# Moving a second norm and part of an edge gather from a tail into the attention before it

## The chip, the cores and the metric

The kernel runs on one core of a Trainium2 chip. The metric is the time of one execution on the device, in microseconds (us). The kernel before was timed three times: 15623.67, 15634.05 and 15639.06 us, median 15634.05. A separate execution was recorded by the hardware profiler; it took 15643.13 us, and its trace spans 15641.4 us.

The engines are named as the profile names them: PE multiplies matrices, DVE is the vector engine, ACT the engine for activation functions, POOL the general-purpose engine (it issues the indirect gathers here), SP the engine that issues the other transfers. Each works through its own queue in program order.

## The reference

The input is four entries of 32 x 96 tokens with 256 features, 3072 tokens per entry and 12288 in all.

- Layer 0 is a group norm, then two Mamba scans (over the 96 positions, then over the 32 variables), and a residual.
- Layer 1 normalizes each token and runs an additive attention within each entry: `e[i,j] = Wa . tanh(q_i + k_j + bh)` with 32 hidden units, a softmax over j, and the sum of the normalized tokens. The result is added to the tokens.
- Then each token is normalized a second time, and a graph part follows: `h = x W_gat` gives 4 heads x 4 experts per token. For each of 1048576 edges (and a loop at each token) a score is formed:

```
e = leaky_relu(a_src[src] + a_dst[dst])
alpha = softmax of e over the edges that share dst
agg[dst] = sum of alpha * h[src]
```

  The edge indices of the reference run over 65536 nodes, and there are only 12288 tokens here. Destinations beyond the tokens are dropped and sources beyond them are clamped to the last token. So few edges need a gather; the rest is counted.
- `agg` is normalized, averaged over heads, the best two of four experts get softmax weights, and each token's output is the weighted sum of expert networks `gelu(x W1 + b1) W2 + b2` (256 to 512 to 256), added to the tokens.

## The kernel before

`whole` (L1701) writes one program in an order fixed by hand for PE, ACT, DVE and POOL (`manual_schedule`); Python generators are advanced in turn, and what each emits lands in the engines' queues in that order.

**The attention.** `Attention.units` (L771) walks 3072 slots, 768 for each entry. In a slot, one `th` (L790, ACT) computes tanh for four queries against all 3072 keys, and PE multiplies an earlier slot's `th` by the weight into scores (L766). Eight slots make a unit of 32 queries, and four units a tile of 128 queries: an entry has 24 tiles of 32 slots. `tile_tail` (L867) ends a tile in six steps, one per slot: `factors`, `factors2`, `factors3` (ACT, `f`, L903), `spread` (POOL, four `sf`, L907), `together` (PE, `po`, L912, needs `sf`) and `outputs` (DVE, and the store of the tile's rows to `x2`). So a tile's end depends on POOL, and PE, in order, meets `po` right behind the scores of a slot.

**The second norm.** `after(b)` (L927) reads an entry's `x2` back in 12 pairs of tiles. It takes inverse roots of all variances with one square root on ACT (L675), and for each pair it normalizes (L680), transposes on PE (L694), stores `xn2T`, multiplies by `W_gat` (L948), forms both score vectors on DVE (L952 to L958) and stores them to the tables `tab_s` (source scores and features, 20 numbers a token) and `tab_a` (destination scores, 4 numbers). For entries 0 to 2 this runs beside the next entry's attention, one step in a slot that has no other use of the one shared PSUM bank (`beside`). For entry 3 it runs after the last attention.

**Beside the attention of the last entries.** `Edges.sort` (L1027) compacts the edge lists on DVE; it ends with the copy of `cnt` (L1162), and then the expert weights are loaded. The list has four parts, one for each entry of the destination, with 108 columns of 128 edges each: `si` and `di` hold the rows of the tables to gather. From the last entry on, `Experts.early` (L1435) computes expert units whose gates are not yet known and keeps the products in DRAM (`kept`). A unit is one expert on one block of 512 tokens. While `after(3)` runs behind the last attention, each of its steps is followed by four steps of early units (L1809).

**The tail.** `tail` (L1518) does the remaining expert units, three steps a unit, with the graph part planned by step number (`at`). `Graph.tables` (L1202) loads both tables, takes the maximum source score over all partitions (`topa`, L1216, POOL) and computes the shift of each destination, `leaky(a_dst + max)`; the score and the shift go to a third table, `tab_d`, 8 numbers a token, which is stored to DRAM. `Graph.gather` (L1245) fetches 12 columns with 24 indirect transfers issued by POOL (L1253), alternately `gs` from `tab_s` and `gd` from `tab_d`, one per column. There are 36 such groups, in the order of entries 3, 2, 0, 1; group m is emitted at step 12 + 4m. Ten steps later `scores` (L1260) forms the weights, `spread` (L1270) builds one-hot matrices (`ol`, `oh`) and products (`rh`, L1284), and `place` (L1289) sums them with PE (`pa`, L1294) into one bank for the entry. After nine groups `finish` (L1299) makes the gates of an entry. Four `gs` and four `gd` buffers exist, so a gather waits for the scores four groups back. A block whose gates are late has its products kept and added afterwards (L1503, `y<-all`).

Of the kernel before, what the change touches and what calls it, by code (L numbers as in the profile page):

```python
# [26 lines left out]
P = 128  # L27
# [17 lines left out]
KQ = TOK // NQT  # L45
LAG = 2
# [15 lines left out]
G0, PART = 4, 8  # L62
# [560 lines left out]
class Attention:  # L623
# [303 lines left out]
    def after(self, b):  # L927

        nc, mv = self.nc, self.state[b]["mv2"]
        N = NT // CT  # L930
        x2 = self.x2[b * TOK:(b + 1) * TOK, :]
        x = self.tiles_of(x2, 0)
        rs = self.inverse_roots(mv)
        yield
        for j in range(N):
# [27 lines left out]
            nc.sync.dma_start(self.tab_a[:, n0:n0 + CT, :], db)  # L963
# [3 lines left out]
class Edges:  # L967
# [6 lines left out]
    def __init__(self, ctx, tc, a):  # L974
# [8 lines left out]
        self.nc.sync.dma_start(self.lanes, a["lanes"])  # L983

# [51 lines left out]
    def sort(self):  # L1036
# [4 lines left out]
        with ExitStack() as ctx:  # L1041
# [124 lines left out]
class Graph:  # L1166
# [4 lines left out]
    def __init__(self, ctx, tc, a, ed, tab_s, tab_a, tab_d, gates):  # L1171
        self.nc, self.ed = tc.nc, ed
        self.tab_s, self.tab_a, self.tab_d, self.gates = tab_s, tab_a, tab_d, gates
# [28 lines left out]
    def tables(self):  # L1202
# [3 lines left out]
        adst = new("adst", [P, NH, 2 * HEADS])  # L1206
        nc.sync.dma_start(hall, self.tab_s)
        nc.sync.dma_start(adst[:, :, 0:HEADS], self.tab_a)
# [5 lines left out]
        top, topa = new("top", [P, HEADS]), new("topa", [P, HEADS])  # L1214
        nc.vector.tensor_reduce(top, hall[:, :, 0:HEADS].rearrange("p n h -> p h n"), AX.X, ALU.max)
# [5 lines left out]
        nc.sync.dma_start(self.tab_d, adst)  # L1221
# [23 lines left out]
    def gather(self, j):  # L1245
        nc, ed = self.nc, self.ed
        gs = self.wk.tile([P, GP, ROW], F32, tag="gs", name="gs", bufs=4)
        gd = self.wk.tile([P, GP, 2 * HEADS], F32, tag="gd", name="gd", bufs=4)
        q, c0 = divmod(j * GP, CQ)
        rows = lambda t: t.rearrange("p n f -> (p n) f")  # L1250
        for u in range(GP):
            for to, table, idx in ((gs, self.tab_s, ed.si), (gd, self.tab_d, ed.di)):
                nc.gpsimd.indirect_dma_start(  # L1253
                    out=to[:, u, :], out_offset=None, in_=rows(table),
                    in_offset=bass.IndirectOffsetOnAxis(ap=idx[:, q, c0 + u:c0 + u + 1], axis=0))
        self.got[j] = gs, gd

    def scores(self, j):
        nc = self.nc
        gs, gd = self.got.pop(j)  # L1260
        e = self.wk.tile([P, GP, HEADS], F32, tag="e", name="e")
        v = self.wk.tile([P, GP, ROW], F32, tag="v", name="v")
        nc.vector.tensor_tensor(e, gs[:, :, 0:HEADS], gd[:, :, 0:HEADS], ALU.add)
        self.leaky(e)
        nc.vector.tensor_tensor(e, e, gd[:, :, HEADS:], ALU.subtract)
# [252 lines left out]
def tail(tc, a, ed, ex, w, tab_s, tab_a, tab_d, gates):  # L1518


    with ExitStack() as ctx:
        gr = Graph(ctx, tc, a, ed, tab_s, tab_a, tab_d, gates)
        ex.open(ctx, w)
        gr.tables()
# [28 lines left out]


# [53 lines left out]
def general_tail(tc, a, x2, xn2T, tab_s, tab_a, tab_d, gates, out, dram):  # L1608

    nc = tc.nc  # L1610
    with ExitStack() as ctx:
# [3 lines left out]
        gr = Graph(gctx, tc, a, none, tab_s, tab_a, tab_d, gates)  # L1615
# [6 lines left out]
        gr.tables()  # L1622
        for _ in gr.own_edges():
            pass
# [77 lines left out]
def whole(tc, a, dram, out):  # L1702
# [10 lines left out]
    tab_a = dram.tile([P, NH, HEADS], F32, tag="tab_a", name="tab_a")  # L1713
    tab_d = dram.tile([P, NH, 2 * HEADS], F32, tag="tab_d", name="tab_d")
    with ExitStack() as ctx:
        actx, lctx, ectx = ExitStack(), ExitStack(), ExitStack()
        with tc.manual_schedule(engines={E.PE, E.Activation, E.DVE, E.Pool}):
# [9 lines left out]
            def steps():  # L1727
# [11 lines left out]
                lists, units = ed.sort(), None  # L1739

                us_v = us_t = 0.0
                while True:
                    us_v = min(us_v, 0.0) + EDGE_US
                    while lists and us_v > 0 and len(ed.todo) < 2:
                        us = next(lists, None)
                        if us is None:
                            lists = None
                            late["w"] = Experts.weights(
                                ectx.enter_context(tc.tile_pool(name="late2", bufs=1)), nc, a)
# [32 lines left out]
            tables = x2, xn2T, tab_s, tab_a, tab_d, late["gates"], out  # L1782
            tail(tc, a, late["ed"], late["ex"], late["w"], *tables[2:6])
# [81 lines left out]
```

## Time and profile before

| what | value |
| --- | --- |
| median of three runs | 15634.05 us |
| the profiled execution's own time | 15643.13 us |
| span of its trace | 15641.4 us |
| PE, DVE, ACT, POOL busy over the span | 75%, 71%, 77%, 58% |
| `cnt` copied, the sort's end | 13617.6 us |
| last score matmul of the attention (L766) | ends near 13991 us |
| first gather of the tail | 14227.4 us |
| last gather of the tail | 15481.3 us |
| last matmul | ends near 15613.9 us |

All times count from the start of the span. The span falls into four stretches that matter here: the work up to the sort's end, the last tiles of the attention (13617 to 14004), the stretch in which only the second norm of entry 3 and early units run (14004 to 14225), and the tail (14225 to the end). A busy share over the whole span mixes them, so each is read alone.

### The profile page before, as it was taken

Reading aid. Unit: us, or ns where it says so; the run is one execution under the profiler, and the core shown is the slowest. Engines: PE = TensorE matmul, PEld = TensorE weight load, DVE = VectorE, ACT = ScalarE, POOL = GpSimd, SP = SyncE. Lnnn points to the kernel's source line nnn. Section 1 sums busy time; section 2 is a strip of 40 time slices with the busy share of each in tenths; the row PEclk is TensorE's granted clock in tenths of the full one; section 3 lists DMA queues with packets and bytes.
Section 4 is the critical chain, followed back from the end, with each engine's and each line's share of the span. In section 5 each row is a group of like instructions: output and inputs, shape, how many; then the busy total and the mean of one; then the engine's idle time right before and its main releaser. Section 6 shows DMA issues by size and latency. Waiting matters only on the chain.

```text
span 15641.4 us, 222408 instructions
## 1 busy us (share of the span) xinstructions
PE 11808.2 (75%) x85872; PEld 5087.3 (33%) x85872; DVE 11045.8 (71%) x15303; ACT 12053.9 (77%) x9331; POOL 9052.0 (58%) x6586
## 2 busy tenths in 40 slices
PE   5666665777777767777777777777778788889988
PEld 2222222222222232222223322222233344446545
DVE  7888888777777787777778876777677733323455
ACT  3443335999999979999998899999979899971211
POOL 4555557777777767777777675777500000004774
PEclk8888886888888888888888888888889999999999
DMA  5666665444445444444444443454310000013223
GB/s 188 203 202 203 199 198 160 149 145 151 148 146 150 154 151 145 145 148 147 148 149 150 151 147 115 143 152 151 121 47 28 17 8 8 21 36 82 43 62 101
DMA packets 1168144, 1959.71 MB, mean 125 GB/s; under 512 B 408545, under 2 KB 612961, under 8 KB 1164897
## 3 DMA queue, kind: packets, MB, share of 16 engines
q1 hardware_dynamic: 1139424, 1939.16, 39.8%
q0 software_dynamic: 27648, 6.25, 0.8%
q8 instruction: 675, 11.06, 0.3%
q14 instruction: 397, 3.24, 0.1%
HBM read 1841.73 MB, written 103.28 MB: 124 GB/s over the span
## 4 chain that ended last, share of the span: by engine, by line
ACT 37%; PE 20%; DVE 17%; POOL 12%; issue 10%; DMA 4%; SPq 0%; DVEq 0%; POOLq 0%; ACTq 0%
ACT th L790 27%; PE pe L766 9%; DVE h L388 6%; ACT dA L371 6%; POOL h L395 4%; POOL gs L1253 3%; POOL gd L1253 3%; PE pv L857 2%; DVE dB L379 2%; ACT pr L841 2%; DMA bB<-bc 2%; PE ptw L848 1%; PE po L1432 1%; POOL ub L305 1%; PE ph L1424 1%
## 5 line engine op out<-in xcount | busy, mean ns | idle before, releaser
L790 ACT ACTIVATE th<-krep,qsel 128x3072 f32<-128x3072 f32 x3072 | 8666.3, 2848 | 327.1 <-PE pe L766 309.7
L766 PE MATMUL pe<-th,wa_blk 128*32 128x384 f32 x49152 | 5118.1, 547 | 1893.1 <-ACT pr L841 1536.3
L395 POOL TENSOR_TENSOR h<-h,bC 128x768 f32<-128x768 f32 x2048 | 3785.0, 1848 | 2561.5 <-DVE h L388 2310.8
L388 DVE TENSOR_TENSOR_SCAN h<-dA,dB 128x384 f32<-128x384 f32 x4096 | 3683.3, 940 | 787.4 <-ACT dA L371 601.8
L766 PEld LDWEIGHTS pe<-th,wa_blk 128*32 128x32 f32 x49152 | 1472.2, 118 | 4581.0 <-issue 1989.1
L379 DVE TENSOR_TENSOR dB<-bB,dtu 128x768 f32<-128x768 f32 x2048 | 1946.2, 950 | 131.7 <-DMA bB<-bc 87.5
L371 ACT ACTIVATE dA<-dt,t_A 128x380 f32<-128x380 f32 x2048 | 1122.1, 570 | 879.6 <-DVE h L388 873.9
L907 POOL TENSOR_SCALAR sf<-sel,f 128x32 f32<-128x32 f32 x384 | 152.5, 421 | 2639.2 <-ACT f L903 2522.0
L371 ACT ACTIVATE dA<-dt,d_A 128x372 f32<-128x372 f32 x2048 | 1097.8, 562 | 557.3 <-DVE h L388 551.8
L414 PE MATMUL py<-h,ident 128*128 128x384 f32 x2176 | 1000.6, 592 | 680.0 <-POOL h L395 678.7
L402 POOL TENSOR_TENSOR h<-h 128x768 f32<-128x768 f32 x752 | 1422.9, 1892 | 46.6
L850 DVE COPY pT<-ptw 128x512 f32<-128x512 f32 (+1 forms) x768 | 425.7, 554 | 1149.6 <-PE ptw L848 1148.4
L857 PE MATMUL pv<-xn,pT 128*32 128x257 f32 x18432 | 1090.6, 384 | 84.3 <-DVE pT L850 83.5
L414 PEld LDWEIGHTS py<-h,ident 128*128 128x128 f32 x2176 | 438.1, 219 | 1243.8 <-POOL h L395 1016.1
L403 POOL TENSOR_TENSOR h<-h 128x384 f32<-128x384 f32 x752 | 803.0, 1068 | 59.0
L404 POOL TENSOR_TENSOR y<-y,h 128x384 f32<-128x384 f32 x752 | 773.7, 1029 | 59.0
L857 PEld LDWEIGHTS pv<-xn,pT 128*32 128x32 f32 x18432 | 584.4, 111 | 638.3 <-DVE pT L850 169.5
L1500 ACT ACTIVATE h<-ph,b 128x512 f32<-128x512 f32 x248 | 165.2, 686 | 702.8 <-PE ph L1424 702.4
L1253 POOL DMA_INDIRECT gs<-tab_s,si x432 | 501.6, 1161 | 131.7 <-issue 127.1
L1253 POOL DMA_INDIRECT gd<-tab_d,di x432 | 487.3, 1128 | 134.7 <-issue 130.1
L309 DVE SCALAR_TENSOR_TENSOR ua<-ub,ua 128x384 f32<-128x384 f32 x256 | 429.2, 1677 | 190.5 <-POOL ub L305 186.3
L1432 PE MATMUL po<-w,h 128*128 128x256 f32 x1984 | 471.9, 393 | 54.7 <-DVE o L1493 38.4
(280 smaller groups left out, 14868.4 us busy)
## 6 DMA issues: line engine op xcount, KB each, us to landing
bB<-bc SPq DMA_DIRECT2D x2048, 384.0 KB
bC<-bc SPq DMA_DIRECT2D x2048, 384.0 KB
x<-x SPq DMA_DIRECT2D x144, 256.0 KB
kept<-ko SPq DMA_DIRECT2D x68, 512.0 KB
all<-kept SPq DMA_DIRECT2D x17, 2048.0 KB
xt<-xn2T SPq DMA_DIRECT2D x59, 512.0 KB
x<-x SPq DMA_DIRECT2D x192, 128.0 KB
xs<-in_xT SPq DMA_DIRECT2D x16, 768.0 KB
```

The lines of the kernel that those rows point to most:

```text
L371: nc.scalar.activation(inner(dA[:, :T]), inner(blk["dt"][:, e, :]), AF.Exp, scale=blk["w"]["A"][:, e, i + s:i + s + 1])
L379: nc.vector.tensor_tensor(dB, blk["bB"].pop(j), z["dtu"].unsqueeze(1).to_broadcast([P, SB, T]), ALU.mult)
L388: nc.vector.tensor_tensor_scan(h[:, s, :], z.pop(("dA", e, i + s))[:, :T], z["dB"][:, s, :], 0.0, ALU.mult, ALU.add)
L395: nc.gpsimd.tensor_tensor(h, h, blk["bC"].pop(j), ALU.mult)
L402: nc.gpsimd.tensor_tensor(h0, h0, h1, ALU.add)
L403: nc.gpsimd.tensor_tensor(h0[:, 0, :], h0[:, 0, :], h0[:, 1, :], ALU.add)
L404: nc.gpsimd.tensor_tensor(y[e], y[e], h0[:, 0, :], ALU.add)
L414: nc.tensor.matmul(z["py"], self.ident, h[:, s, :], start=(i == 0), stop=(i == DS - 1))
L766: nc.tensor.matmul(pe[q * QU:(q + 1) * QU, j, :KQ // 2], self.wa[:, k, :], th[:, c0:c0 + KQ // 2], start=(k == 0), stop=(k == NK - 1))
L790: nc.scalar.activation(th, s["krep"], AF.Tanh, bias=s["qsel"][:, col:col + 1])
L857: nc.tensor.matmul(pv[q * QU:(q + 1) * QU, :C + 1], pT[:, i, q * QU:(q + 1) * QU], s["xn"][:, q * NK + i, :], start=(i == 0), stop=(i == N ...
L1253: nc.gpsimd.indirect_dma_start(out=to[:, u, :], out_offset=None, in_=rows(table), in_offset=bass.IndirectOffsetOnAxis(ap=idx[:, q, c0 + u: ...
```

## The change

1. **The last entry's second norm in four parts.** `after` takes a range of tiles. For entry 3 it is appended three times beside its own attention, for tiles 0 to 7, 8 to 15 and 16 to 21, twelve slots after the last slot of the part (slots 268, 524 and 716 of 768). Only tiles 22 and 23, one pair, are left for behind the attention. Each part takes its own square roots.
2. **Destination scores in a table per entry, without the shift.** `tab_a` becomes four DRAM tables, `tab_d` is not used in the normal case, and `di` becomes a row within an entry's table (four small DVE instructions more in the sort). The shift is formed after the gather, from the gathered score and `topa`, with two DVE instructions more for each group of 12 columns.
3. **Gathered beside the last attention.** `gd` becomes one tile for all 432 columns. When the sort has ended, each slot of the attention emits three gathers of entries 0, 1 and 2, until 324 are done. The 108 of entry 3 stay in the tail, beside their `gs`. So the tail issues 540 gathers in place of 864.
4. **Tail order.** Group 0 is gathered ahead of `tables`, group m at step 4m (m from 1), with scores at step 10 + 4m. `tables` is called after the plan has been laid out.

In the built programs the number of expert units done up to the last score matmul is the same: 20 complete, and the hidden half of the 21st. Behind it the kernel before does 13 hidden halves and 14 output halves more as early units and 62 units in the tail; the changed one does 3 and 4 more, and 72 in the tail. The blocks with kept products go from 17 to 14.

```diff
+AFTER = (0, 8), (8, 16), (16, 22), (22, 24)
-G0, PART = 4, 8
+G0, PART = 10, 8
-    def inverse_roots(self, mv):
+    def inverse_roots(self, mv, t0=0, t1=NT):
         rs = self.rows.tile([P, NT], F32, tag="lrs", name="lrs")
-        self.nc.scalar.activation(rs, mv[:, :, 1], AF.Sqrt, bias=self.eps)
-        self.nc.vector.reciprocal(rs, rs)
+        some = rs[:, t0:t1]
+        self.nc.scalar.activation(some, mv[:, t0:t1, 1], AF.Sqrt, bias=self.eps)
+        self.nc.vector.reciprocal(some, some)
...
-            if b and col == LAG + 10:
+            if b and col == LAG + 10 and b < B:
                 side.append(self.after(b - 1))
+            if b == B - 1:
+                side += [self.after(b, t0, t1) for t0, t1 in AFTER[:-1]
+                         if col == t1 * P // R_ATT + LAG + 10]
...
-        side.append(self.after(B - 1))
+        side.append(self.after(B - 1, *AFTER[-1]))
...
-            nc.sync.dma_start(self.tab_a[:, n0:n0 + CT, :], db)
+            nc.sync.dma_start(self.tab_a[b][:, j * CT:(j + 1) * CT, :], db)
...
+    def places(self, pool, tab_a):
+        self.gd = pool.tile([P, 4, CQ, HEADS], F32, tag="gd", name="gd")
+        self.tab_a, self.have = tab_a, set()
+
+    def gather(self, q, c):
+        if (q, c) not in self.have:
+            self.have.add((q, c))
+            self.nc.gpsimd.indirect_dma_start(
+                out=self.gd[:, q, c, :], out_offset=None,
+                in_=self.tab_a[q].rearrange("p n f -> (p n) f"),
+                in_offset=bass.IndirectOffsetOnAxis(ap=self.di[:, q, c:c + 1], axis=0))
...
+                if rows is self.di:
+                    v.tensor_scalar(lo, lo, float(NT) / NH, None, ALU.mult)
+                    for q in range(1, 4):
+                        part = hi[:, q * CQ:(q + 1) * CQ]
+                        v.tensor_scalar(part, part, float(-q * NT), 0.0, ALU.add, ALU.max)
...
-        nc.sync.dma_start(self.tab_d, adst)
...
         for u in range(GP):
-            for to, table, idx in ((gs, self.tab_s, ed.si), (gd, self.tab_d, ed.di)):
-                nc.gpsimd.indirect_dma_start(
-                    out=to[:, u, :], out_offset=None, in_=rows(table),
-                    in_offset=bass.IndirectOffsetOnAxis(ap=idx[:, q, c0 + u:c0 + u + 1], axis=0))
+            nc.gpsimd.indirect_dma_start(
+                out=gs[:, u, :], out_offset=None, in_=rows,
+                in_offset=bass.IndirectOffsetOnAxis(ap=ed.si[:, q, c0 + u:c0 + u + 1], axis=0))
+            ed.gather(q, c0 + u)
...
-        nc.vector.tensor_tensor(e, e, gd[:, :, HEADS:], ALU.subtract)
+        nc.vector.tensor_tensor(sh, gd, self.topa.unsqueeze(1).to_broadcast([P, GP, HEADS]), ALU.add)
+        self.leaky(sh)
+        nc.vector.tensor_tensor(e, e, sh, ALU.subtract)
...
-            t = 3 * G0 + PART * m // 2
-            at(t, lambda j=j: gr.gather(j))
-            t += 10
+            t = G0 + PART * m // 2
+            if m < 1:
+                gr.gather(j)
+            else:
+                at(max(0, t - 10), lambda j=j: gr.gather(j))
             at(t, lambda j=j: gr.scores(j))
...
+                            ed.places(pool, tab_a)
+                            columns = [(q, c) for q in range(B - 1) for c in range(CQ)]
...
                     while units and us_t > 0:
                         us_t -= next(units) or 0.0
+                    for _ in range(3 if columns else 0):
+                        ed.gather(*columns.pop(0))
                     yield
```

More of the change, by code (lines that the diff above doesn't have):

```diff
@@ L925, in tile_tail, with after @@
         return [factors, factors2, factors3, spread, together, outputs]
-    def after(self, b):
+    def after(self, b, t0=0, t1=NT):
         nc, mv = self.nc, self.state[b]["mv2"]
-        N = NT // CT
+        j0, N = t0 // CT, t1 // CT
         x2 = self.x2[b * TOK:(b + 1) * TOK, :]
-        x = self.tiles_of(x2, 0)
-        rs = self.inverse_roots(mv)
+        x = self.tiles_of(x2, j0)
+        rs = self.inverse_roots(mv, t0, t1)
         yield
-        for j in range(N):
+        for j in range(j0, N):
             rowsd = slice(b * TOK + j * CT * P, b * TOK + (j + 1) * CT * P)
@@ L1166, with __init__ @@
 class Graph:
-    def __init__(self, ctx, tc, a, ed, tab_s, tab_a, tab_d, gates):
+    def __init__(self, ctx, tc, a, ed, tab_s, tab_a, gates):
         self.nc, self.ed = tc.nc, ed
-        self.tab_s, self.tab_a, self.tab_d, self.gates = tab_s, tab_a, tab_d, gates
+        self.tab_s, self.tab_a, self.gates = tab_s, tab_a, gates
         pool = lambda name, bufs, **k: ctx.enter_context(tc.tile_pool(name=name, bufs=bufs, **k))
@@ L1205, in tables @@
         self.hall = hall = new("hall", [P, NH, ROW])
-        adst = new("adst", [P, NH, 2 * HEADS])
+        adst = self.adst = new("adst", [P, NH, 2 * HEADS])
         nc.sync.dma_start(hall, self.tab_s)
-        nc.sync.dma_start(adst[:, :, 0:HEADS], self.tab_a)
+        for q in range(4):
+            nc.sync.dma_start(adst[:, q * NT:(q + 1) * NT, 0:HEADS], self.tab_a[q])
         last = self.last = new("last", [P, ROW])
@@ L1214, in tables @@
         top, topa = new("top", [P, HEADS]), new("topa", [P, HEADS])
+        self.topa = topa
         nc.vector.tensor_reduce(top, hall[:, :, 0:HEADS].rearrange("p n h -> p h n"), AX.X, ALU.max)
@@ L1247, in gather @@
         gs = self.wk.tile([P, GP, ROW], F32, tag="gs", name="gs", bufs=4)
[L1248 removed]
         q, c0 = divmod(j * GP, CQ)
[L1250 removed]
+        rows = self.tab_s.rearrange("p n f -> (p n) f")
         for u in range(GP):
[L1252 to L1256 removed]
+            nc.gpsimd.indirect_dma_start(
+                out=gs[:, u, :], out_offset=None, in_=rows,
+                in_offset=bass.IndirectOffsetOnAxis(ap=ed.si[:, q, c0 + u:c0 + u + 1], axis=0))
+            ed.gather(q, c0 + u)
+        self.got[j] = gs
     def scores(self, j):
         nc = self.nc
[L1260 removed]
+        gs = self.got.pop(j)
+        q, c0 = divmod(j * GP, CQ)
+        gd = self.ed.gd[:, q, c0:c0 + GP, :]
         e = self.wk.tile([P, GP, HEADS], F32, tag="e", name="e")
+        sh = self.wk.tile([P, GP, HEADS], F32, tag="sh", name="sh")
         v = self.wk.tile([P, GP, ROW], F32, tag="v", name="v")
[L1263 removed]
+        nc.vector.tensor_tensor(e, gs[:, :, 0:HEADS], gd, ALU.add)
         self.leaky(e)
[L1265 removed]
+        nc.vector.tensor_tensor(sh, gd, self.topa.unsqueeze(1).to_broadcast([P, GP, HEADS]), ALU.add)
+        self.leaky(sh)
+        nc.vector.tensor_tensor(e, e, sh, ALU.subtract)
         self.weighted(e, v, gs[:, :, HEADS:], GP)
@@ L1515, in outputs_tile, with tail @@
         return self.io.tile([P, NQ, NEXP, C], F32, tag="all", name="all")
-def tail(tc, a, ed, ex, w, tab_s, tab_a, tab_d, gates):
+def tail(tc, a, ed, ex, w, tab_s, tab_a, gates):
     with ExitStack() as ctx:
-        gr = Graph(ctx, tc, a, ed, tab_s, tab_a, tab_d, gates)
+        gr = Graph(ctx, tc, a, ed, tab_s, tab_a, gates)
         ex.open(ctx, w)
-        gr.tables()
         PER = NBLK_X // B
@@ L1552, in tail @@
                 ready[q] = t + 5
+        gr.tables()
         first = {i: n for n, (i, e) in reversed(list(enumerate(units)))}
@@ L1605, in tail, with general_tail @@
                         ex.store(i, to[n - 1])
-def general_tail(tc, a, x2, xn2T, tab_s, tab_a, tab_d, gates, out, dram):
+def general_tail(tc, a, x2, xn2T, tab_s, tab_a, gates, out, dram):
     nc = tc.nc
@@ L1614, in general_tail @@
         none.cnt = None
-        gr = Graph(gctx, tc, a, none, tab_s, tab_a, tab_d, gates)
+        gr = Graph(gctx, tc, a, none, tab_s, tab_a, gates)
+        tab_d = dram.tile([P, NH, 2 * HEADS], F32, tag="tab_d", name="tab_d")
         const = gctx.enter_context(tc.tile_pool(name="hc", bufs=1))
@@ L1622, in general_tail @@
         gr.tables()
+        nc.sync.dma_start(tab_d, gr.adst)
         for _ in gr.own_edges():
@@ L1712, in whole @@
     tab_s = dram.tile([P, NH, ROW], F32, tag="tab_s", name="tab_s")
-    tab_a = dram.tile([P, NH, HEADS], F32, tag="tab_a", name="tab_a")
-    tab_d = dram.tile([P, NH, 2 * HEADS], F32, tag="tab_d", name="tab_d")
+    tab_a = [dram.tile([P, NT, HEADS], F32, tag=f"tab_a{b}", name=f"tab_a{b}") for b in range(B)]
     with ExitStack() as ctx:
@@ L1738, in steps @@
                 ex = late["ex"] = Experts(ectx, tc, x2, xn2T, late["gates"], out, dram)
-                lists, units = ed.sort(), None
+                lists, units, columns = ed.sort(), None, []
                 us_v = us_t = 0.0
@@ L1747, in steps @@
                             lists = None
-                            late["w"] = Experts.weights(
-                                ectx.enter_context(tc.tile_pool(name="late2", bufs=1)), nc, a)
+                            pool = ectx.enter_context(tc.tile_pool(name="late2", bufs=1))
+                            late["w"] = Experts.weights(pool, nc, a)
+                            ed.places(pool, tab_a)
+                            columns = [(q, c) for q in range(B - 1) for c in range(CQ)]
                         else:
@@ L1781, in whole @@
             actx.close()
-            tables = x2, xn2T, tab_s, tab_a, tab_d, late["gates"], out
-            tail(tc, a, late["ed"], late["ex"], late["w"], *tables[2:6])
+            tables = x2, xn2T, tab_s, tab_a, late["gates"], out
+            tail(tc, a, late["ed"], late["ex"], late["w"], *tables[2:5])
             ectx.close()
```

## The prediction

> **What bounds the kernel now.** I read three stretches, from the table of stages first (columns: length; busy time of PE, weight loads, DVE, ACT, POOL; granted clock; DMA).
>
> ```profile
> 13860.00:13960.00 100.00, 84.46 (x792) 38.26 (x794) 16.60 (x31) 95.66 (x41) 1.36 (x4) 0.91 0.04 13
> 14150.00:14200.00 50.00, 46.29 (x179) 30.56 (x180) 19.09 (x42) 3.82 (x2) 0.00 (x0) 1.00 0.28 86
> 14400.00:14500.00 100.00, 99.69 (x318) 60.01 (x317) 41.12 (x56) 23.34 (x30) 79.27 (x69) 1.00 0.24 39
> 15000.00:15100.00 100.00, 81.72 (x243) 47.41 (x242) 55.50 (x98) 18.87 (x25) 79.58 (x68) 0.92 0.40 108
> ```
>
> The last attention is bound by ACT (96 of 100 us) and POOL is idle. In the stretch of the second norm PE is nearly full. In the tail PE is full at first, then drops to 82 of 100, while POOL issues 68 to 70 gathers per 100 us throughout. The groups of the tail say who waits:
>
> ```profile
> L1253 POOL DMA_INDIRECT gs<-tab_s,si x432 | 501.6, 1161 | 131.7 <-issue 127.1 <-DMA gs<-tab_s,si 4.6
> L1263 DVE TENSOR_TENSOR e<-gs,gd 128x48 f32<-128x48 f32 x36 | 7.7, 213 | 289.1 <-DMA gd<-tab_d,di 280.7 <-DMA gs<-tab_s,si 8.4
> L1294 PE MATMUL pa<-rh,ol 128*128 128x480 f32 x864 | 395.7, 604 | 73.2 <-DVE rh L1284 73.2
> ```
>
> POOL waits for nothing but its own issue; DVE waits 281 us for gathers; PE waits for DVE. The chain that ended last agrees: from 14228 to 15468 it consists of gathers and their transfers. POOL's timeline shows the price of one:
>
> ```profile
> 14407.25 0.94 POOL L1253 DMA_INDIRECT gs<-tab_s,si  x1 [0.30 <-issue]
> 14408.50 1.14 POOL L1253 DMA_INDIRECT gd<-tab_d,di  x1 [0.30 <-issue]
> 14409.95 2.06 POOL L1253 DMA_INDIRECT gs<-tab_s,si  x1 [0.30 <-issue]
> ...
> 14417.48 2.66 POOL L1253 DMA_INDIRECT gs<-tab_s,si  x1 [0.30 <-issue]
> 14420.44 0.94 POOL L1253 DMA_INDIRECT gd<-tab_d,di  x1 [0.31 <-issue]
> ```
>
> Undisturbed it is 0.94 + 0.30 = 1.25 us from start to start. Slow ones come in bursts. Laying DVE's timeline beside POOL's over the whole tail, the 429 gathers with no DVE work beside them took 0.94 us; those beside only `ko<-po` (37) or `o<-po` (5), which read PSUM, also 0.94; those beside only `rh` (50), two SBUF inputs, 2.34 on average.
>
> **Prices.** A unit's period in PE at full clock, and `pa`, from PE's timeline: equal places of two units are 13.77 us apart, and the next group starts 3.22 us after eight records of `pa`, of which a group of 12 columns has 24.
>
> ```profile
> 15570.66 3.62 PE L1432 MATMUL po<-w,h 128*128 128x256 f32 x16
> ...
> 15584.43 3.62 PE L1432 MATMUL po<-w,h 128*128 128x256 f32 x16
> ```
>
> So a half unit is 6.88 us, a group's `pa` 9.66, and four tail steps (4/3 unit and one group) 4/3 x 13.77 + 9.66 = 28.0 us. A group of 24 gathers took (15482.2 - 14227.4)/36 = 34.9. Check: 62 units and 36 groups are 854 + 348 = 1202 us of PE; it took 15613.9 - 14224.8 = 1389, so 187 were lost. By gathers: first scores stood at step 22 (101 us of PE), their data was there after 40, a lead of 61, against which each further group loses 6.9: 35 x 6.9 - 61 = 181. The rule holds within 6 us, and I use it for the changed kernel.
>
> **Part 1, gathers beside the attention.** Three gathers a slot are 3 x 1.25 = 3.7 us of POOL in a slot of some 3 us: POOL becomes the slower. POOL works in order, and the `sf` of each tile stand between the gathers: in the built program 3, 97, 96, 96 and 33 gathers, with a tile's `sf` behind the first three, behind each 97 or 96, and at the end. Behind a late `sf` waits `po` (L912), and PE, in order, with it; then the three `th` buffers fill and ACT stops.
>
> ```profile
> 13618.61 1.36 POOL L907 TENSOR_SCALAR sf<-sel,f 128x32 f32<-128x32 f32 x4 [101.48 <-ACT f L903]
> 13712.56 1.36 POOL L907 TENSOR_SCALAR sf<-sel,f 128x32 f32<-128x32 f32 x4 [92.58 <-ACT f L903]
> 13814.26 1.36 POOL L907 TENSOR_SCALAR sf<-sel,f 128x32 f32<-128x32 f32 x4 [100.35 <-ACT f L903]
> 13917.55 1.36 POOL L907 TENSOR_SCALAR sf<-sel,f 128x32 f32<-128x32 f32 x4 [101.93 <-ACT f L903]
> 14000.94 1.36 POOL L907 TENSOR_SCALAR sf<-sel,f 128x32 f32<-128x32 f32 x4 [82.03 <-ACT f L903]
> ```
>
> The first gather waits for the sort's last products (`cnt` is copied at 13617.6). With the first three gathers the first `sf` ends near 13623; 289 gathers at 1.25 and two `sf` at 1.45 bring the fourth tile's `sf` to 13987, against 13917.6: 69 late. Some 6 us are taken up by the distance from `sf` to `po` (13620.0 to 13626.0 in the first of these tiles). Then 33 gathers, 41 us, fit into the 83 before the last `sf`. Delay of the attention's end: 63 us. The price in that stretch is not in the trace; its ends are 1.25 (undisturbed, and beside PSUM reads) and 3.2 (the longest, 2.9 + 0.3). DVE is busy 17 to 22 of 100 us there, nearly all with PSUM reads (`pT`, `nb`, `h`, `pvs`), so I take 1.25. If all of its 18 us cost as the tail's burst does (4.9 us per group beside some 8.5 us of DVE work), it would be 1.40, and the delay 106.
>
> A rule speaks against this. The Trainium skill, "SBUF — State Buffer", section "A bandwidth-pool intuition that's wrong (but worth ruling out)", has a DMA issued from GpSimd go from 620 to 3100 ns beside a DVE copy that locks the shared port. If each of the 31 to 42 DVE instructions per 100 us cost those 2.5 us, some 125 instructions would add about 310 us as an estimate, and the kernel would end near 15810. The rows of gathers beside `ko` and `o` show no such cost for PSUM reads, and the sum goes by them.
>
> **Part 2, the norm's parts beside the attention.** Moved are 11 of 12 pairs; for the 12 the stretch behind the attention shows PE 7.2 + 11.5 us, DVE about 28, ACT 0.3 + 1.28 us of table load. Each part adds a square root and two table loads (2.9 us) to ACT, which sets the pace. The third part (slots 716 on) runs while `sf` waits for POOL, and costs nothing as long as the gathers bind. For the first two, 8 pairs: PE 12.5, DVE 19, ACT 5.8; nothing if all lies in gaps, 37 if all is on the path. ACT's 5.8 are surely on it, PE has 12 to 18 idle in 100 and DVE more: I take 12. SP's loads and stores move past others in its queue, where transfers take 3 of 100 us of the DMA engines; nothing, or, if late, part of the same 37.
>
> **Part 3, the stretch behind the attention.** From 14004.5 it took 220.3: 12 hidden and 14 output halves (179), and the norm's 18.7, with a factor 1.115. Left are 2 hidden and 4 output halves: 41.3 x 1.115, and 3 for a gelu behind the square root: 50. The ten units go to the tail.
>
> **Part 4, the tail.** 72 units and 36 groups: 991 + 348 = 1339 of PE at full clock, which 14400 to 14500 shows it holds when fed. The first nine groups still have 24 gathers. Group 0 needs the last table store, with 13 hidden matmuls (11 us) and two output halves (14) still before the tail, so it starts 21 before it and is there 12 after its start. `topa` now queues behind it on POOL, and DVE's shift and ACT's exponent behind `topa`: 8 us, covered by the first hidden half, about 3 left for PE. Scores begin at step 10 (46 us). The ninth group is there at 12 + 30 + 33 + 6 x 34.9 = 284, PE wants it at 46 + 8 x 28 = 270: 14 lost. After that 12 gathers take 12 x 1.25 + 4.9 = 20 < 28, and POOL runs ahead. With the four `finish` (4.4 us lost where one falls, 14500 to 14600: 95.6 of 100 busy) I take 30 for all losses, between 10 and 60. `tab_d` goes with its store (3.3 us of POOL waiting); two DVE instructions more per group (0.21 us each, 15 in all) lie under PE. Tail: 1369.
>
> **Part 5, the end.** Before, two kept blocks are added after the last matmul: 27.5 us. Now the last kept block is done ten units earlier; what remains is `o`, two additions and a store: 1.7 + 6.5 = 8.
>
> **Sum.** 14004.5 + 63 + 12 + 50 + 1369 + 8 = 15506.5 against the span of 15641.4. The profiled execution took 1.7 more than its span and 9 more than the median: 15500, faster by 0.86%.
>
> **The rivals.** *Slower: the port.* If DVE's attention work slows each gather, the fourth `sf` moves by 289 times the difference. From 1.73 us a gather on, the delay is 201 and eats the gain; at 2.6 (as beside `rh`) the time is 15890. For it: the bursts; against: 0.94 beside PSUM reads. 0.08; between 1.40 and 1.73 (15545 to 15640) 0.05.
> *Same: PE stays starved.* If not the gathers but DVE's order (73 + 38 + 16 us of PE waits) set the loss, the tail keeps 187 in place of 30: 15657. For it: these waits; against: DVE itself waits 289 us for gathers there. 0.05.
> *Faster still: the late `sf` is absorbed* by buffers, as PE and ACT run ahead: 15437. Against: 6 us from `sf` to `po`. 0.04.
>
> **The numbers.** The forecast has 0.78. Its own range: below, parts 12 to 0, losses 30 to 10, stretch 50 to 44: 15460; above, 1.40 a gather (+43), parts 37 (+25), losses 60 (+30): 15600. The range takes a little of the neighbours, 15445 to 15610. A measurement tells about 0.2% from no change: faster 0.87, same 0.05, slower 0.08.
>
> **What would show it.** Right: POOL busy from 13618 without gaps to the last-but-one `sf`, gathers at 1.25; `po` L912 waiting for `sf` three times, 25 to 31 us; the attention ending 60 to 110 later; PE over 95 of 100 in the tail after the ninth group; no additions of `y<-all` at the end. Wrong: gathers over 1.4 in the attention, PE waiting for `rh` throughout, or the first two parts costing over 40.

## The result, and the profile after

The changed kernel took 15547.59 us, the median of four runs (15542.97 to 15553.6), against 15636.56 for the kernel before, run beside it (15623.67 to 15652.53). The ratio is 0.9943, with a 95% interval of 0.9926 to 0.996. The forecast was 15500 with a range of 15445 to 15610. The profiled execution took 15547.17 us, with a span of 15545.4.

One thing must be known to read the numbers below. This comparison and the last experiment ran on chips on which the kernel before takes 15626 to 15637 us. The eleven other runs were on three other chips, on which the same kernel before takes 15866 to 15896. Each time is therefore set against the kernel before on its own chip. I call them the first and the second kind of chip, going by the time of the kernel before alone; what sets the two apart is not known. The sign of the change is not the same on both, and most of the experiments turned to the reason.

The stages first, for the changed kernel on the first kind of chip (columns as before: length; busy time of PE, weight loads, DVE, ACT, POOL; granted clock; DMA share; GB/s):

```profile
13700.00:13800.00 100.00, 57.33 (x542) 24.53 (x534) 12.83 (x24) 68.96 (x31) 76.34 (x83) 0.80 0.14 15
14200.00:14300.00 100.00, 99.38 (x316) 59.42 (x315) 42.09 (x60) 22.06 (x29) 79.58 (x68) 1.00 0.19 41
14300.00:14400.00 100.00, 89.64 (x269) 52.93 (x268) 36.15 (x54) 18.88 (x25) 78.97 (x70) 0.93 0.23 36
14900.00:15000.00 100.00, 93.61 (x281) 54.42 (x282) 58.01 (x115) 22.85 (x30) 42.83 (x37) 0.97 0.15 40
15300.00:15400.00 100.00, 100.00 (x351) 66.45 (x350) 56.78 (x118) 20.34 (x30) 0.00 (x0) 1.00 0.39 137
```

In the attention ACT has fallen from 96 to 69 of 100 us and POOL is the busy engine. In the tail PE keeps 90 to 100 of 100, and at the end POOL has nothing left to issue. POOL's timeline at the second late `sf`, PE's at the same moment, and PE's chain of waits in 13600 to 14150 show the price in the attention:

```profile
13742.55 0.95 POOL L998 DMA_INDIRECT gd<-tab_a,di  x1 [0.30 <-issue]
13743.54 1.36 POOL L912 TENSOR_SCALAR sf<-sel,f 128x32 f32<-128x32 f32 x4
13745.06 1.01 POOL L998 DMA_INDIRECT gd<-tab_a,di  x1 [0.16 <-issue]
```

```profile
13743.98 1.61 PE L917 MATMUL po<-pvs,sf 128*32 128x257 f32 x6 [28.99 <-POOL sf L912]
```

```profile
PE po L917 <- POOL sf L912: 62.9, 3, 29.0
PE pe L768 <- ACT pr L846: 39.6, 12, 11.0
```

`sf` stands without any idle time between two gathers: POOL came to it when the 97 gathers ahead were out. PE stood 29.0 us at `po` for it, 20.2 and 13.8 at the next two tiles, 62.9 us in all. The groups of the tail (14122 to the end) give the other side:

```profile
L1275 POOL DMA_INDIRECT gs<-tab_s,si x423 | 503.3, 1190 | 340.9 <-DVE v L1220 217.9 <-issue 117.2 <-DMA gs<-tab_s,si 4.9
L1322 PE MATMUL pa<-rh,ol 128*128 128x480 f32 x864 | 380.4, 585 | 35.2 <-DVE rh L1312 35.2
L1289 DVE TENSOR_TENSOR e<-gs,gd 128x48 f32<-128x48 f32 x36 | 7.3, 202 | 40.6 <-DMA gd<-tab_a,di 31.5 <-DMA gs<-tab_s,si 9.1
```

POOL now waits 218 us for a free `gs` buffer, which it never did before; DVE's wait for gathers falls from 289 to 41 us and PE's wait for `rh` from 73 to 35. Once the first nine groups are through, the gathers no longer set the pace of the tail.

### The profile page after: what moved, and what is told of

It is laid out like the page before. It is cut to its first block, busy times and chain, and to the rows that moved or that the text cites. A ratio compares the mean times of both kernels' runs of the same rounds, so it can differ in the third digit from the quotient of the medians.

```text
span 15545.4 us, 222373 instructions
## 1 busy us (share of the span) xinstructions
PE 11739.5 (76%) x85872; PEld 5061.5 (33%) x85872; DVE 11037.6 (71%) x15342; ACT 12076.6 (78%) x9370; POOL 9002.8 (58%) x6586
## 4 chain that ended last, share of the span: by engine, by line
ACT 36%; PE 25%; DVE 17%; POOL 9%; issue 8%; DMA 4%; SPq 0%; DVEq 0%; POOLq 0%; ACTq 0%
ACT th L792 26%; PE pe L768 9%; DVE h L389 6%; ACT dA L372 6%; POOL h L396 4%; PE po L1460 3%; POOL gd L998 2%; PE ph L1452 2%; DVE dB L380 2%; PE pv L862 2%; DMA bB<-bc 2%; PE pa L1322 2%; ACT pr L846 2%; PE ptw L853 1%; POOL ub L306 1%
## 5 line engine op out<-in xcount | busy, mean ns | idle before, releaser
L998 POOL DMA_INDIRECT gd<-tab_a,di x432 | 429.6, 994 | 232.0 <-issue 132.4
L1460 PE MATMUL po<-w,h 128*128 128x256 f32 x2304 | 526.8, 382 | 15.6 <-ACT h L1528 7.2
```

What stands on the lines that cost most here:

```text
L1460: self.nc.tensor.matmul(po[:, q, :], h[:, f, (q0 + q) * P:(q0 + q + 1) * P], w2[:, f, :], start=(f == 0), stop=(f == FC - 1))
```

## Experiments

In the tables and texts "PE in the window" is PE's busy time in 13600 to 14000, the last four tiles of the attention. In the kernel before it is 349.3 of 400 us.

**First set: the parts alone, and two repairs.** They ran on a chip where the kernel before took 15895.74 us (13 runs, 15846.17 to 15916.34).

`e1_sf_dve`, the late `sf` moved to another engine for the last entry:

```diff
-                nc.gpsimd.tensor_scalar(sf[:, u, :], self.sel, f[:, u:u + 1], None, ALU.mult)
+                (nc.vector if b == B - 1 else nc.gpsimd).tensor_scalar(
+                    sf[:, u, :], self.sel, f[:, u:u + 1], None, ALU.mult)
```

> The four sf of a tile of the last entry go from POOL to DVE; all else as in the changed kernel. If the attention ends 68 us later (last po of the attention at 14072.6 against 14004.5) because sf stands in POOL's queue behind three gathers a slot, its end goes back to 14004 to 14012, the tail starts near 14054 to 14062 and keeps its loss of 70 us of PE: 15470 to 15490 us. If the gathers slow the attention in another way (DVE or the transfers beside them), the attention still ends 50 us or more late and the time stays within 15 us of 15547.

Measured: 16037.8 us (4 runs), 1.0095 (1.0072 to 1.0118) of the kernel before on that chip. The repair made it slower, where I expected it faster. The window, and PE's timeline inside it:

```profile
13600.00:14000.00 400.00, 108.29 (x413) 29.52 (x414) 9.15 (x24) 40.54 (x17) 292.38 (x293) 0.54 0.11 15
```

```profile
13844.14 0.80 PE L768 MATMUL pe<-th,wa_blk 128*32 128x384 f32 x1 [2.00 <-issue]
13846.93 0.80 PE L768 MATMUL pe<-th,wa_blk 128*32 128x384 f32 x1 [2.00 <-issue]
13849.74 0.80 PE L768 MATMUL pe<-th,wa_blk 128*32 128x384 f32 x1 [2.00 <-issue]
13852.53 0.80 PE L768 MATMUL pe<-th,wa_blk 128*32 128x384 f32 x1 [2.00 <-issue]
13855.33 0.80 PE L768 MATMUL pe<-th,wa_blk 128*32 128x384 f32 x1 [2.00 <-issue]
```

PE is busy 108 of 400 us and ACT 41, while POOL issues 293 gathers, one every 1.25 us up to 13840 and one every 1.40 us from there on. The matmuls do not wait for data ("issue" means that the profile shows nothing they wait for); they start one every 2.80 us, with a weight load half way between, so one PE instruction every 1.40 us. The last of the early gathers starts at 14043.4, and in 14080 to 14100 PE runs 184 matmuls in 20 us again. Nothing in the traces of the first kind of chip looks like this.

`e2_split_only`, the norm in parts and the new tables, but no gather beside the attention:

```diff
-                            columns = [(q, c) for q in range(B - 1) for c in range(CQ)]
+                            columns = []
```

> The norm of the last entry in four parts, but no gather beside the attention: all 864 gathers in the tail. If the tail of before was bound by the gathers, it stays so: attention ends near 14004, tail starts near 14054, 36 groups of 34.9 us end near 15290, and after the last group's scores 66 of 216 steps of PE remain, some 300 us: 15590 to 15625 us. If splitting the norm is what gains and the gathers were hidden anyway, PE sets the tail: 14054 + 1339 + 70 + 8, some 15475.

Measured: 15893.44 us in one run, inside the spread of the kernel before there. The attention is undisturbed (its last `po` starts by 14007, against 14004.2 in the kernel before on the first kind of chip). The tail is not: from 14060 to 15876, at 0.43 us for a `ph`, 0.215 for a `po` and 0.4025 for a `pa`, 475 us held no PE work, against 182 in the tail of the kernel before on the first kind. As this run and the next came to the second kind, how the gain on the first kind divides between the parts of the change was not measured.

`e3_gather_only`, the early gathers with the norm in one piece:

```diff
-AFTER = (0, 8), (8, 16), (16, 22), (22, 24)
+AFTER = (0, 24),
```

> Gathers beside the attention, but the last entry's norm whole behind it, as before. Attention ends near 14072; the stretch behind it takes 220 us again; the tail has 62 units and 36 groups, 1202 us of PE at full clock, and loses some 50 to 75; at the end kept blocks are added for up to 28 us: 15565 to 15595 us. If the split is worth nothing, 15547 within 10.

Measured: 16030.52 us in one run, 135 above the kernel before there. PE in the window: 185.2, with 195 gathers.

`e4_quarters`, the changed kernel with the tail's quarters in another order, the one without early gathers last:

```diff
-QUARTERS = 3, 2, 0, 1
+QUARTERS = 2, 0, 1, 3
```

> Entries are gathered in the order 2, 0, 1, 3, so the nine groups with 24 gathers come last, when POOL is ahead, and topa stands behind 12 gathers. If the changed tail loses 26 us of PE at its ninth group because POOL is behind, and 9 at its start because topa is behind group 0, these go and nothing comes in their place at the end (the last nine groups need 314 us of POOL from a start four groups ahead, against 336 of PE): 15505 to 15525 us. If the starvation only moves to the last nine groups, 15540 to 15555.

Measured: 15931.83 us (10 runs), 1.003 (1.0018 to 1.0041). PE in the window: 177.9, with 195 gathers. So on this chip each kernel with gathers beside the attention was slower than the one without. PE had least in the window where the gathers ran without pause: the late `sf`, which I had counted as a cost, was here a pause that let the other engines on.

**Second set: the changed kernel itself, and fewer gathers a slot.** Another chip, the kernel before at 15865.88 us (8 runs, 15850.2 to 15895.72). `a_after` is the changed kernel without an edit.

> The changed kernel itself, without any edit, because the chip of the first four experiments ran even the kernel before in 15896 us, against 15635 for the first measurements. Theory S (other engines starve for instructions while GpSimd issues gathers, and how much differs between chips): where the kernel before takes about 15635, this one takes 15547 again; where it takes about 15896, this one lies between the order-only edit (15932) and the gathers-only edit (16031), at 15940 to 16000, slower than before. Rival (the edits themselves cost what the first four runs showed, and the chip only adds a constant): before minus 88 on either chip, so 15808 on the second.

Measured: 16007.7 us (4 runs), 1.0087 (1.0071 to 1.0104): slower than before, by 142 us. Theory S had given 15940 to 16000, a little less than this, the rival 15808. Its window, and the DMA queues' instruction rows from 13620 to 14000 (packets, MB, share):

```profile
13600.00:14000.00 400.00, 185.02 (x1321) 66.83 (x1323) 29.79 (x58) 150.75 (x63) 189.16 (x203) 0.67 0.11 20
```

```profile
q8 instruction: 9, 0.15, 0.2%
q14 instruction: 1, 0.01, 0.0%
```

The same kernel on the first kind of chip has this in the same stretches:

```profile
13600.00:14000.00 400.00, 298.45 (x2780) 135.75 (x2784) 67.94 (x140) 323.88 (x137) 291.50 (x316) 0.87 0.18 32
```

```profile
q8 instruction: 21, 0.34, 0.4%
q14 instruction: 4, 0.03, 0.0%
```

All four busy columns ahead of POOL's fall to between 44% and 62% of what they are there. On the timeline of this run PE's rate falls some 10 to 17 us after a run of gathers begins, and recovers some 10 us after its end (in `e1_sf_dve`, behind 293 gathers, it takes 30).

`e5_both`, the two repairs `e1_sf_dve` and `e4_quarters` together (both diffs above):

> Two edits: the last entry's sf on DVE, and the tail's quarters in the order 2, 0, 1, 3. Theory of the lock (GpSimd's order holds sf up by 68 us; the quarter without early gathers starves the tail by 26 us): where the kernel before takes about 15635, 15445 to 15470, about 90 below the changed kernel. Theory S, where it takes about 15896: the gathers run without the pauses at sf, so this is no better than sf on DVE alone less the 26, 16000 to 16040, above the changed kernel. If S holds in a weaker form on the first kind of chip too: 15480 to 15540 there, with fewer matmuls per 100 us in the stretch 13620 to 14000 than the kernel before (792).

Measured: 15946.58 us (4 runs), 1.006 (1.0039 to 1.008). PE in the window: 106.3, as low as in `e1_sf_dve`. The time is below what S gave (16000 to 16040); so the order of quarters seems to be worth more than the 26 us that I had taken for it (1.006 here against 1.0095 in `e1_sf_dve`, each set against the kernel before on its own chip).

`e6_two`, two gathers a slot:

```diff
-                            columns = [(q, c) for q in range(B - 1) for c in range(CQ)]
+                            columns = [(q, c) for q in (2, 0, 1) for c in range(CQ)]
...
-                    for _ in range(3 if columns else 0):
+                    for _ in range(2 if columns else 0):
```

> Two gathers a slot in place of three (quarters 2, 0, 1): 2.5 us of GpSimd in a slot of 3 us, so sf is not held up, and some 260 of the 324 gathers still lie beside the attention. Theory of the lock, where the kernel before takes about 15635: 15480 to 15500. Theory S, where it takes about 15896: the same gathers hold up the same engines, so near the changed kernel, within 40 us of it.

Measured: 15928.98 us (5 runs), 1.0042 (1.0027 to 1.0056), 79 below the changed kernel where S gave at most 40. `e7_one` is the same edit with `1` in place of `2`:

> One gather a slot: about 130 of the 324 beside the attention, the others in the tail. Theory of the lock, where the kernel before takes about 15635: no late sf (minus 68), but 16 more groups with 24 gathers in the tail (16 x 6.9 = 110, less the lead that nine groups with 12 make, 9 x 8 = 72): 15515 to 15560. Theory S, where it takes about 15896: the attention suffers from 130 gathers and not from 324, so this one is nearest to the kernel before, 15890 to 15930, below the changed kernel.

Measured: 15841.37 us in one run, lower than S gave (15890 to 15930) and 9 below the lowest of the eight runs of the kernel before. Its window:

```profile
13600.00:14000.00 400.00, 269.55 (x2457) 116.35 (x2450) 59.81 (x123) 290.72 (x123) 96.86 (x109) 0.85 0.11 29
```

Taking the 349.6 of an undisturbed window on such chips (`e9_memset` and `e10_hw`, below), each gather cost nearly the same PE time:

| run | gathers in the window | PE in the window | lost per gather |
| --- | --- | --- | --- |
| `e5_both` | 295 | 106.3 | 0.82 |
| `e1_sf_dve` | 293 | 108.3 | 0.82 |
| `a_after` | 195 | 185.0 | 0.84 |
| `e3_gather_only` | 195 | 185.2 | 0.84 |
| `e4_quarters` | 195 | 177.9 | 0.88 |
| `e6_two` | 165 | 212.5 | 0.83 |
| `e7_one` | 97 | 269.5 | 0.83 |

That the loss goes by the number of gathers was rival S2 of the next set. One gather a slot does not mean that they come evenly: POOL runs its queue as fast as it can, 32 gathers in 40 us, and then waits for the next `sf`.

**Third set: what in a gather does it.** A third chip, the kernel before at 15884.82 us (7 runs, 15847.95 to 15909.56). `e8_pause` puts a write on POOL behind each early gather (`sf` on DVE as in `e1_sf_dve`):

```diff
+                            pause = pool.tile([P, 1024], F32, tag="pause", name="pause")
...
-                    for _ in range(3 if columns else 0):
+                    for _ in range(1 if columns else 0):
                         ed.gather(*columns.pop(0))
+                        nc.gpsimd.memset(pause, 0.0)
```

> One gather a slot, each followed by a write of 128x1024 zeros on GpSimd as a pause (an estimated 1.2 to 2 us), and the last entry's sf on DVE, so that the gathers come evenly and not in bursts of 32. Theory S1 (an engine's next block of instructions gets through only in a gap between gathers): with a gap behind each gather the attention runs as without gathers, about 350 us of TensorE in 13600 to 14000 against 269 with one gather a slot without pause. Rival S2 (each gather costs the other engines the same, 0.7 to 0.8 us of TensorE, whenever it comes): about 260 us for some 120 gathers. Where the kernel before takes about 15635 both give 15510 to 15560.

Measured: 15747.86 us (4 runs), 0.9916 (0.9895 to 0.9936): 137 us faster than before, on the kind of chip on which the change itself was 142 slower. The write took 0.97 us, where I had estimated 1.2 to 2. POOL's timeline, and the windows of the attention and of the tail's start:

```profile
13801.51 0.95 POOL L999 DMA_INDIRECT gd<-tab_a,di  x1 [0.17 <-issue]
13802.45 0.97 POOL L1801 MEMSET pause<- 128x1024 f32 x1
13803.59 0.95 POOL L999 DMA_INDIRECT gd<-tab_a,di  x1 [0.17 <-issue]
```

```profile
13600.00:14000.00 400.00, 348.25 (x3238) 154.06 (x3235) 87.69 (x183) 370.75 (x157) 251.52 (x262) 0.94 0.14 34
14100.00:14200.00 100.00, 17.99 (x49) 10.49 (x48) 2.47 (x8) 5.56 (x7) 72.14 (x77) 0.61 0.09 10
```

With 131 gathers, each 2.08 us after the one before, PE has 348 of 400 us and has lost nothing. S2 gave 260. In the same trace, at the start of the tail, 77 gathers in a row without pauses leave PE 18 of 100 us. So the chip is of the second kind and the pause is what differs. Whether it is the write itself or only the wider spacing (2.08 us in place of 1.25) that helps was not separated.

`e9_memset` asks whether a busy POOL is enough: three such writes a slot, `sf` on DVE, and all gathers in the tail.

```diff
-                        ed.gather(*columns.pop(0))
+                        columns.pop(0)
+                        nc.gpsimd.memset(pause, 0.0)
```

> GpSimd is given three writes of 128x1024 zeros a slot in place of the three gathers (which all stay in the tail), sf of the last entry on DVE: it is busy and moves nothing. Theory S (the gathers' transfers or descriptors starve the other engines): the attention runs as in the kernel before, TensorE some 350 us in 13600 to 14000. Rival P (a busy GpSimd itself holds the others up, by the memory port or otherwise): TensorE falls below 300 there.

```profile
13600.00:14000.00 400.00, 349.65 (x3313) 154.05 (x3306) 92.66 (x186) 375.07 (x159) 308.95 (x324) 0.96 0.11 33
```

Measured: 15860.23 us in one run. POOL is busy 309 of 400 us, more than with gathers, and PE has 349.7: rival P falls.

`e10_hw` asks whether small transfers are enough: the same number of bytes in as many pieces, from fixed rows, issued by SP.

```diff
-                        ed.gather(*columns.pop(0))
+                        q, c = columns.pop(0)
+                        nc.sync.dma_start(ed.gd[:, q, c, :], tab_a[q][:, c % NT, :])
```

> The three gathers a slot are replaced by three plain transfers of the same 128 x 16 bytes each, issued by SyncE from fixed rows of the same table (the true gathers all stay in the tail and write the same places later). Theory S3 (descriptors that GpSimd writes are what starves the others): TensorE some 340 to 350 us in 13600 to 14000, sf not late, no waits for issue. Rival S4 (small transfers as such, whoever issues them, hold up the transfers of instructions): TensorE 180 to 230 there, as in the changed kernel on such a chip.

```profile
13600.00:14000.00 400.00, 349.64 (x3305) 154.21 (x3298) 82.34 (x167) 375.05 (x159) 6.82 (x20) 0.96 0.17 35
```

Measured: 15840.77 us in one run. The DMA engines are busier than with gathers (0.17 against 0.11), and PE has 349.6: rival S4 falls. What held the other engines up was a stream of indirect gathers from POOL, issued one right behind the other. The transfers of `e10_hw` differ from the gathers in two things, the issuing engine and the fixed rows; plain transfers issued by POOL were not tried, so which of the two matters is open.

The kernels of `e9_memset` and `e10_hw` have all 864 gathers in the tail, as the kernel before has. In 14100 to 14200, with 77 gathers in a row, PE has 18.6 and 19.0 of 100 us there. So the kernel before very likely pays too on such chips. The 230 to 270 us that it takes longer there fit a tail held up in this way (475 us without PE work in `e2_split_only`, against 182), though no trace of it was taken on one of them.

**Last: a version built from this.** A write behind every fourth gather, in the attention and in the tail; two gathers a slot; `sf` of the last entry on DVE; the quarters in the order 2, 0, 1, 3.

```diff
+    def gap(self):
+        self.n += 1
+        if self.n % 4 == 0:
+            self.nc.gpsimd.memset(self.pause, 0.0)
...
+            ed.gap()
             ed.gather(q, c0 + u)
```

> A gap (one write of 128x1024 zeros, 0.97 us on GpSimd) behind every fourth gather, beside the attention and in the tail; two gathers a slot in the order of quarters 2, 0, 1; sf of the last entry on DVE; the tail's quarters in the order 2, 0, 1, 3. Theory S1 (instructions get through in the gaps): a gather is 1.25 + 0.83/4 = 1.46 us, 262 of them take 382 us from 13606, TensorE has 345 to 355 us in 13600 to 14000 and no waits for issue over a microsecond; the tail is 14010 + 50 + 1339 + 8 plus 30 to 120 of losses (a group of 24 gathers takes 35 us against 28 of TensorE, after a lead from the 22 groups with 12), so 15440 to 15530 on every chip, some 350 to 440 below the kernel before where that takes about 15885. Rival S2 (each gather costs the others the same): TensorE 150 to 200 us in 13600 to 14000, and the time above 15880. Rival S5 (a gap behind every fourth is too rare, the one behind every gather was needed): TensorE 220 to 320 there, the time 15600 to 15850.

It came to a chip of the first kind (the kernel before at 15625.74 us, 9 runs). Measured: 15500.08 us (5 runs, 15496.76 to 15501.67), 0.9918 (0.9905 to 0.9932). That is 126 us below the kernel before, where the change alone was 89 below. So it is the fastest version seen on this kind of chip (the two ratios' intervals overlap a little, 0.9926 to 0.9932), though it gives no verdict on S1 against S5, which differ only on the second kind. What it does bear on is the late `sf`. Its attention window, PE's waits behind 14060, and two of its tail's stages:

```profile
13600.00:14000.00 400.00, 348.74 (x3278) 154.03 (x3271) 86.99 (x177) 371.19 (x157) 311.59 (x327) 0.94 0.18 35
```

```profile
PE pa L1331 <- DVE rh L1321: 60.3, 20, 10.3
PE po L1469 <- DVE o L1530: 9.1, 1, 9.1
```

```profile
14100.00:14200.00 100.00, 99.68 (x310) 58.63 (x309) 42.24 (x61) 22.66 (x29) 81.77 (x71) 1.00 0.27 64
15000.00:15100.00 100.00, 77.66 (x221) 45.55 (x220) 52.46 (x98) 15.53 (x21) 83.20 (x78) 0.88 0.31 83
```

With `sf` off POOL's queue, 0.8 us of waiting for `sf` is left. From the `po` at 13616.9 to the last one at 14002.1 it takes 385 us; the same stretch takes 378 in the kernel before (13626.0 to 14004.2) and 446 in the changed one (13626.0 to 14072.2). The new order takes away the loss at the start of the tail (99.7 of 100 busy). It comes back at the end, where groups of 24 gathers and their writes keep POOL at 83 of 100: counted as above, 80 of the tail's 92 us of loss lie between 14600 and 15200, 51 of them in the last 200.

## Why the prediction was right, and where it was off

By its own steps, on the kind of chip it was made for:

| step | predicted | measured |
| --- | --- | --- |
| pace of the early gathers | 1.25 us | (13743.54 - 13623.1)/97 = 1.24 |
| fourth tile's `sf` | 13987 | 13987.42 |
| `po` waiting for `sf` | three times, 25 to 31 us | 29.0, 20.2 and 13.8 us, 62.9 in all |
| delay by the gathers | 63 | 68.0, with the norm's third part in it |
| the norm's first two parts | 12 | 13.7 |
| arrival ahead of these parts | as before | 13.7 earlier |
| end of the attention | 14004.5 + 63 + 12 = 14079.5 | 14072.6 |
| stretch behind the attention | 50 | 49.4 |
| tail to the last matmul | 1369 (1339 and 30 of losses) | 1415.2 |
| end | 8 | 8.2 |
| span | 15506.5 | 15545.4 |

**Gathers beside the attention: right.** The delay came from POOL's order: the fourth `sf` came 70 us later than before (13987.42 against 13917.55), and from the `po` at 13626.0 to the last one PE took 68.0 us more. In `e11_gaps`, on the same kind of chip with `sf` on DVE and 262 gathers in the window, this stretch is 7 us longer than before, and PE does not wait for POOL in it. The rival "the late `sf` is absorbed" is out, and so are the 6 us that I took off for the distance from `sf` to `po`: nearly all of the delay reached PE. The waits of 25 to 31 us each did not fit my own sum, since three of them would make 75 to 93; their total of 62.9 is the 63 of the sum. The rule that spoke against the change, in the Trainium skill, "SBUF — State Buffer", section "A bandwidth-pool intuition that's wrong (but worth ruling out)", has a DMA issued from GpSimd take five times as long beside a DVE copy that holds the shared port. The median gather of `gd` took 952 ns here, beside 140 DVE instructions in 400 us, so that no such stretch is seen with these copies, most of which read PSUM. The sum went by the row, and rightly.

**The norm's first two parts: 12 us, measured 8 to 14.** The first part begins behind 12400. From the `po` of the tile ahead of it to the `po` at 13626.0, PE took 1613.9 us in the changed kernel (12012.1 to 13626.0) and 1600.2 in the kernel before (12025.8 to 13626.0). `e3_gather_only`, whose norm stays in one piece, took 1600.0; the eleven other runs with the norm in parts took 1607.5 to 1614.0. So the term holds. It does not show in the attention's end, and that is luck: this execution came to the first of these tiles 13.7 us earlier than the trace of before, 20.9 earlier already at 2727, ahead of all that the change moves. What brought this shift is not shown, and the forecast does not contain it. It explains why the attention ended 7 us earlier than forecast, though both of its terms came out larger.

**The tail's losses: the term that was mis-sized.** I took 30 us, between 10 and 60; they came to 70 of missing PE work (work counted from records), or 76 of time. Three places carry it. The start cost 9.4 where I had said 3:

```profile
14135.43 0.56 DVE L1244 TENSOR_TENSOR adst<-adst,topa 128x384 f32<-128x384 f32 x1 [11.67 <-POOL topa L1241]
14142.59 4.63 PE L1460 MATMUL po<-w,h 128*128 128x256 f32 x10 [7.16 <-ACT h L1528]
```

`topa` came 24 gathers later in POOL's queue, DVE waited 11.7 us for it, and PE then stood 7.2 us at `po` for ACT's `h`. I had named this chain and thought it covered by the first hidden half. The ninth group's starvation was 14; in 14300 to 14500 26.4 are lost, some 19 of them up to 14440, where the chain that ended last consists of gathers until the ninth group has landed (14418), and 5 in 14440 to 14460, beside the first finishing of an entry (`agg` at 14450.9). The finishing of entries and the rest were 16, and from 14700 on 34 are lost, in pieces of up to 10 in 100 us, while PE waits 21.5 us for `rh`. The three stretches of 100 us with a finishing (from 14700, 14900 and 15200) hold 23 of the 34; how that divides between the finishing and DVE's order I have not taken apart. The sign "PE over 95 of 100 in the tail after the ninth group" fails in two of these stretches, at 94.3 and 93.6. The rival of DVE's order has its grain here: PE's 35 us of waits for `rh` stayed when the gathers stopped binding, though not the 187 that it would have needed.

The sum of the differences: -7 at the attention's end (+5 for the gathers, +2 for the norm, -14 for the earlier arrival), -1 in the stretch, +46 in the tail, which is the 39 between 15506.5 and 15545.4. The other 9 between 15500 and 15547.59 come from the step from span to median: I took 9 off because the profiled execution of the kernel before was that much slower than its median, and the changed kernel's was not.

**What the prediction did not contain.** On the second kind of chip the change costs 142 us. None of the rivals is this mechanism. The nearest, the port, had POOL's gathers slowed by the other engines; here the gathers nearly keep their pace (1.25 us, in `e1_sf_dve` later 1.40) and the other engines are slowed. No row of the trace of before could have shown it, since that trace is from a chip that does not behave so, and a range from one chip's trace holds for such a chip alone.

## What to carry to other kernels

An engine that works in order and is "idle" in a stretch may still hold short instructions that others wait for: count how many new ones stand ahead of each of them, because that count times their pace gave the place of the fourth `sf` to within 1 us (13987 against 13987.42). Put the work that others wait for on another engine, or ahead of the stream, rather than behind it. Before a stream of indirect gathers goes beside dense work, measure it on more than one chip, and break the stream with another instruction on the issuing engine: at one gather a slot, a write of 0.97 us behind each raised PE's busy time in the window from 269.5 us to 348.3, an undisturbed one's.

## What the runs showed of the hardware that I had not expected

- On three of the chips, from 10 to 17 us after a run of back-to-back indirect gathers begins, the other engines' instructions start late with nothing to wait for; PE goes down to one instruction every 1.40 us, and its clock is granted at 0.54 over the window of `e1_sf_dve`. Where the first measurement and the last experiment ran, such a stream has no such effect.
- It costs 0.82 to 0.88 us of PE for each gather in this attention, in runs of 32 gathers and of 293 alike. A busy POOL without gathers (`e9_memset`) and small transfers from SP (`e10_hw`) cost nothing, and gathers 2.08 us apart with a write between them (`e8_pause`) cost nothing either.
- I had explained it by blocks of instructions that can't get through. The traces do not bear that part out. One packet of the q8 instruction queue comes for every 250 to 280 PE instructions (matmuls and weight loads in 13600 to 14000) in all runs, so that few packets are as well the effect of few instructions. In `e1_sf_dve` such a packet comes at 13848.5, and PE's step of 2.80 us is the same before and after it, in the lines shown above. What is slow is the start of each instruction; through what the gathers reach it stays open, and so does what distinguishes the two kinds of chip. Whether a write behind every fourth gather is enough on the second kind of chip was not measured.
